# A four-tap convolution moved from diagonal matrices on TensorE to products on ScalarE and sums on GpSimd, and row loads moved to SP's queue

## The chip, the cores and the metric

The kernel runs on one core of a Trainium2 chip. The core has a matrix engine (TensorE, called PE in the profile, with its weight loads as PEld), a vector engine (VectorE, DVE), an activation engine (ScalarE, ACT), a general engine (GpSimd, POOL) and a sequencer that here only issues DMAs (SyncE, SP). Each works through its own queue in order; semaphores tie the queues together. The metric is device time in microseconds (us) of one execution. Lower is better.

## The reference, cut to what matters

The program is a chain of four blocks on x of shape 8 x 512 x 256, all in float32, each added to its input: latent attention, a feed-forward block with 4-bit quantisation, a Mamba block that runs in both directions, and the same feed-forward block again. The change lies in the Mamba block:

```python
h = _layernorm(x, gamma, beta)
xs, z = jnp.split(h @ in_w, 2, axis=-1)              # 512 channels each
y_fwd = _ssm_dir(xs, conv_w, ...)                    # and once more on xs[:, ::-1]
...
# _ssm_dir:
xc = silu(causal_depthwise_conv(xs, conv_w, conv_b)) # four taps per channel
dt, B_ssm, C_ssm = split(xc @ xproj_w, [64, 80])     # 64, 16 and 16 columns
dt = softplus(dt @ dt_w + dt_b)
dA = exp(dt[..., None] * A);  dBu = dt[..., None] * B_ssm[:, :, None, :] * xc[..., None]
h = dA * h + dBu                                     # along time, 16 states per channel
y = einsum('bdn,bn->bd', h, C_ssm) + xc * D_skip
```

So every channel gets a convolution of four taps over time, with a bias and a silu, in each of two directions. B and C are 16 rows each over the 512 time steps, and every channel needs all of them.

## The kernel before, in words

Channels lie on the 128 partitions and time (T = 512) along the free axis. The 512 channels are four tiles of 128 (m = 0 to 3). The work of the eight batch entries b is written as three threads: attention (`thread_a`), the feed-forward blocks together with the front and the end of Mamba (`thread_b`), and the scan (`thread_s`). Their steps are interleaved, so the scan of batch b runs beside the attention of batch b+3 and the Mamba front of batch b+1. The scan of batch 0 can only begin when the attention, the feed-forward block and the Mamba front of batch 0 are done.

The order on every engine is not that of the program text. At the end `issue_in_order` (L138) plans the whole kernel: it takes a cost for each instruction, a rank from what depends on it, and rings of buffers per tag, and writes an order for each engine, SP included. The engines then run these orders as they stand, each instruction waiting for its semaphores, with all that is queued after it.

The Mamba front is `mamba_pre` (L929 on). For each m, PE multiplies by in_w, ACT writes the result to one of two constant tiles `xs` with three columns of zeros on either side (L953), and `conv` (L917) runs once for each direction d. There are 8 x 4 x 2 = 64 convolutions. Before the change a convolution loads four 128 x 128 diagonal matrices (`dg`, 256 KB) from DRAM, where `prep_mamba` has put them at the start (L910 to L915); PE multiplies the four shifted views of xs by them, summing in PSUM (L924); ACT takes a tanh of half the sum and adds 1 (L925, L926); DVE makes the last product from PSUM (L927). The result goes to DRAM (`scr["xc"]`, L958). The tiles `dg` and the result both come from the ring tmpB, which has three buffers (TC = 3).

`ssm_prep` loads the convolved channels back (L1012), multiplies by xproj_w, and writes the 32 rows of B and C to DRAM as `bcd` (L1021). It also makes dt; four of its steps are long operations on POOL.

The scan (`ssm`, L1064) goes over d, m and pairs of states n, 512 times in all. One iteration multiplies u by the two B rows on DVE (L1079), has ACT make two exponentials in PSUM (L1082), scans twice on DVE (L1084 forward, L1086 backward), multiplies by the two C rows on POOL (L1093), and has PE sum over states by transposes (L1096). The B rows and the C rows of a pair, spread over all partitions, are 512 KB each; `load_rep` (L1052) loads them into the rings rep0 and rep1 of three buffers, two iterations ahead. With CQ = 0 both are issued from ACT's queue (L1056). The load of a convolved tile for the skip term (L1092) is issued there too. Every other DMA is issued from SP.

Of the kernel before, what the change touches and what calls it, by code (L numbers as in the profile page):

```python
# [11 lines left out]
F32 = mybir.dt.float32  # L12
# [4 lines left out]
AF = mybir.ActivationFunctionType  # L17
ALU = mybir.AluOpType
AX = mybir.AxisListType

P = 128
T = 512
# [6 lines left out]
ND = INNER // P  # L29
NS = 16  # L30
# [31 lines left out]
DMA_LAT = 2300  # L62
# [75 lines left out]
def issue_in_order(tc, traced, rings):  # L138


    ops = [i for i in traced if i.ins or i.outs]
    ops = [i for i in ops if any(True for _ in accesses(i))]
    acc = [list(accesses(i)) for i in ops]
    n = len(ops)
# [14 lines left out]
    turns, owner, waiting, behind, after = {}, {}, {}, [[] for _ in ops], [[] for _ in ops]  # L159
# [16 lines left out]
    succ = [[] for _ in ops]  # L176
# [19 lines left out]
    dma = [type(i).__name__ == "InstDMACopy" for i in ops]  # L196
    rank = [0.0] * n
    for k in reversed(range(n)):
        rank[k] = costs[k][1] * (1.2 if ops[k].engine == mybir.EngineType.DVE else 1) + DMA_LAT * dma[k] + max([rank[j] for j in succ[k] + behind[k]], default=0.0)
    at = [0.0] * n  # L200
    ready, later, free, last, gone, taken = {}, {}, {}, {}, {}, 0.0
    lines, flying = [0.0] * 16, [0.0] * 8
# [65 lines left out]
def tile_hybrid(ctx: ExitStack, tc: tile.TileContext, w: dict, consts: bass.AP, out: bass.AP):  # L268
    nc = tc.nc
# [14 lines left out]
    def const(shape, dt, tag):  # L284
        return cp.tile(shape, dt, tag=tag, name=tag)
# [7 lines left out]
    def work(shape, dt, tag, bufs=2):  # L293
        cnt[0] += 1
        return ringed(tag, bufs, wk.tile(shape, dt, tag=tag, name=f"{tag}_{cnt[0]}", bufs=bufs))
# [4 lines left out]
    def psum(tag="pb"):  # L300
        cnt[0] += 1
        tag = BMAP.get(tag, tag)
        return ringed(tag, BANKS[tag], ps.tile([P, 512], F32, tag=tag, name=f"{tag}_{cnt[0]}", bufs=BANKS[tag]))
# [559 lines left out]
    Dh = const([P, 2, ND], F32, "Dh")  # L863
    cw = const([P, 2, ND, 4], F32, "cw")
    cb = const([P, 2, ND], F32, "cb")
    cbh = const([P, 2, ND], F32, "cbh")
    dg_d = dr.tile([2, ND, P, 4, P], F32, tag="dgd", name="dg_d", bufs=1)
    TH = T // 2
    xsb = [const([P, 3 + T + 3], F32, f"xs{i}") for i in range(2)]
    for i in range(2):  # L870
# [4 lines left out]
    def prep_mamba():  # L875
        gb = work([P, 2, 2], F32, "gb", 1)
        nc.sync.dma_start(gb[:, 0, :], w["gamma"].rearrange("(a p) -> p a", p=P), allow_slow_non_contiguous=True)
        nc.sync.dma_start(gb[:, 1, :], w["beta"].rearrange("(a p) -> p a", p=P), allow_slow_non_contiguous=True)
        o = psum()
        win = [work([P, 2 * INNER], F32, "dt", NDT) for _ in range(2)]  # L880
        for ct in range(2):
            nc.sync.dma_start(win[ct], w["in_w"][ct * P : (ct + 1) * P, :])
        for m in range(8):
            for ct in range(2):
                PE.matmul(o[:, m : m + 1], win[ct][:, m * P : (m + 1) * P], gb[:, 1, ct : ct + 1],
                          start=(ct == 0), stop=(ct == 1))
        V.tensor_copy(bin_, o[:, :8])
        V.tensor_scalar(binh, bin_, 0.5, None, ALU.mult)
        for ct in range(2):
            V.tensor_scalar(win[ct], win[ct], gb[:, 0, ct : ct + 1], None, ALU.mult)  # L890
            nc.sync.dma_start(win_d[:, :, ct, :].rearrange("m p n -> p m n"), win[ct].rearrange("p (m n) -> p m n", m=8))
        wout = work([P, ND, C], F32, "rep0", RB)
        nc.sync.dma_start(wout, w["out_w"].rearrange("(a p) n -> p a n", p=P))
        V.tensor_scalar(wout, wout, 0.5, None, ALU.mult)
        nc.sync.dma_start(wout_d, wout)
        for d, sx in enumerate(("", "_b")):
            wxp = work([P, 2, T], F32, "tmpA", TA).rearrange("p a t -> p (a t)")[:, : ND * 96].rearrange("p (m n) -> p m n", m=ND)
            nc.sync.dma_start(wxp, w["xproj_w" + sx].rearrange("(a p) n -> p a n", p=P))
            V.tensor_scalar(wxp, wxp, 0.5, None, ALU.mult)
            V.tensor_scalar(wxp[:, :, DTR : DTR + NS], wxp[:, :, DTR : DTR + NS], 0.5, None, ALU.mult)  # L900
            nc.sync.dma_start(wxp_d[d], wxp)
            nc.sync.dma_start(Aneg[:, d], w["A_log" + sx].rearrange("(a p) n -> p a n", p=P))
            nc.sync.dma_start(Dh[:, d, :], w["D_skip" + sx].rearrange("(a p) -> p a", p=P), allow_slow_non_contiguous=True)
            nc.sync.dma_start(cw[:, d], w["conv_w" + sx].rearrange("(a p) k -> p a k", p=P))
            nc.sync.dma_start(cb[:, d, :], w["conv_b" + sx].rearrange("(a p) -> p a", p=P), allow_slow_non_contiguous=True)
        S.activation(Aneg, Aneg, AF.Exp)
        V.tensor_scalar(Aneg, Aneg, -1.0, None, ALU.mult)
        V.tensor_scalar(Dh, Dh, 0.5, None, ALU.mult)
        V.tensor_scalar(cbh, cb, 0.5, None, ALU.mult)
        for d in range(2):  # L910
            for m in range(ND):
                dg = work([P, 4, P], F32, "tmpB", TC)
                for k in range(4):
                    S.activation(dg[:, k, :], ident, AF.Copy, scale=cw[:, d, m, k : k + 1])
                nc.sync.dma_start(dg_d[d, m], dg)  # L915

    def conv(d, m, xs, dst):  # L917

        dg = work([P, 4, P], F32, "tmpB", TC)
        nc.sync.dma_start(dg, dg_d[d, m])  # L920
        o = psum()
        for k in range(4):
            at = k if d == 0 else 6 - k
            PE.matmul(o, dg[:, k, :], xs[:, at : at + T], start=(k == 0), stop=(k == 3))  # L924
        S.activation(dst, o, AF.Tanh, bias=cbh[:, d, m : m + 1], scale=0.5)  # L925
        S.activation(dst, dst, AF.Identity, bias=1.0)  # L926
        V.scalar_tensor_tensor(dst, o, cb[:, d, m : m + 1], dst, ALU.add, ALU.mult)  # L927

    def mamba_pre(src, scr):  # L929
        xn = work([P, NT, C], F32, "fxn", 1)  # L930
# [74 lines left out]
    def ssm_prep(b, d, c, scr):  # L1005

        sx = ("", "_b")[d]
        if c == 0:
            us = []
            for i in range(2):  # L1010
                us.append(work([P, 2, T], F32, "u", NU))
                nc.sync.dma_start(us[i], scr["xc"][4 * d + 2 * i : 4 * d + 2 * i + 2].rearrange("m p t -> p m t"))  # L1012
            wxp = work([P, 2, T], F32, "tmpA", TA).rearrange("p a t -> p (a t)")[:, : ND * 96].rearrange("p (m n) -> p m n", m=ND)
            nc.sync.dma_start(wxp, wxp_d[d])
            o = psum("a")
            for m in range(ND):
                mm(o[:96, :], wxp[:, m, :], us[m // 2][:, m % 2, :], start=(m == 0), stop=(m == ND - 1))
            S.copy(dbt[:DTR, :], o[:DTR, :])
            S.copy(dbt[96:, :], o[DTR:96, :])
            bcd = dr.tile([NS, 2, T], F32, tag="bcd", name=f"bcd_{b}_{d}", bufs=4)  # L1020
            nc.sync.dma_start(bcd.rearrange("n k t -> k n t"), dbt[96:, :])  # L1021
            fronts[(b, d)] = us, bcd
            yield
        us, bcd = fronts[(b, d)]
        u = us[c]
        wdt = work([DTR + 1, 2 * P], F32, "wdt", 1)
        cs = slice(2 * c * P, (2 * c + 2) * P)
        nc.sync.dma_start(wdt[:DTR, :], w["dt_w" + sx][:, cs])
        nc.sync.dma_start(wdt[DTR : DTR + 1, :], w["dt_b" + sx][cs].rearrange("(o n) -> o n", o=1))
        dt = work([P, 2, T], F32, "dt", NDT)  # L1030
        prep[(b, d, c)] = dt, u, bcd
        ex = work([P, 2, T], F32, "tmpA", TA)
        for e in range(2):
            o = psum("a")
            PE.matmul(o, wdt[:, e * P : (e + 1) * P], dbt[: DTR + 1, :], start=True, stop=True)
            S.activation(dt[:, e, :], o, AF.Relu)
            S.activation(ex[:, e, :], o, AF.Abs)
            yield
        S.activation(ex, ex, AF.Exp, scale=-1.0)
        lg = work([P, 2, T], F32, "tmpA", TA)  # L1040
        S.activation(lg, ex, AF.Ln, bias=1.0)
        yield
        G.tensor_tensor(dt, dt, lg, ALU.add)
        S.activation(lg, ex, AF.Identity, bias=1.0)
        S.activation(lg, lg, AF.Identity, bias=neg1[:, 0:1])
        yield
        G.tensor_tensor(ex, ex, lg, ALU.subtract)
        G.tensor_tensor(dt, dt, ex, ALU.add)
        G.tensor_tensor(u, dt, u, ALU.mult)
        yield  # L1050

    def load_rep(b, d, m, n, k):  # L1052

        rep = work([P, 2, T], F32, f"rep{k}", RB)
        src = fronts[(b, d)][1][2 * n : 2 * n + 2, k, :]
        (S, nc.sync)[CQ * k].dma_start(rep, src[None].to_broadcast([P, 2, T]))  # L1056
        return rep

    todo_rep = [(b, d, m, n) for b in range(B) for d in range(2) for m in range(ND) for n in range(NS // 2)]
    todo_c = list(todo_rep)  # L1060
    reps, repc = [], []
    CQ = 0

    def ssm(b, d, scr):  # L1064


        for m in range(ND):
# [8 lines left out]
            for n in range(NS // 2):  # L1076
# [12 lines left out]
                    repc.append(load_rep(*todo_c.pop(0), 1))  # L1089
                if n == 2:  # L1090
                    xp = work([P, T], F32, "xp", 1)
                    S.dma_start(xp, scr["xc"][4 * d + m])  # L1092
                G.tensor_tensor(h, h, rc, ALU.mult)  # L1093
                for e in range(2):
                    for i in range(NT):
# [143 lines left out]
```

## Time and profile before

| | us |
|---|---|
| median of 3 runs | 4006.74 (4004.24 to 4007.3) |
| the profiled execution, own time | 4021.45 |
| its span, first to last instruction | 4019.6 |
| first and last L1079 (scan) | 604.3 and 3884.1 |
| first and last L924 (convolution) | 497.0 and 3461.4 |

| engine | busy us | share of the span | instructions |
|---|---|---|---|
| PE | 3217.1 | 80% | 12964 |
| PEld | 1838.2 | 46% | 12964 |
| DVE | 2957.9 | 74% | 3803 |
| ACT | 1738.8 | 43% | 2989 |
| POOL | 2107.4 | 52% | 1714 |

The mean granted clock of TensorE was 0.872 of full speed. The DMA engines moved 898.12 MB in 570642 packets, with a mean busy share of 0.70.

The busy time is that of instructions that compute. Issuing a DMA and waiting for a semaphore hold an engine's queue but do not count as busy. A row of the groups gives a line of the code, the engine, the operation, out<-in by tile names, shapes and count, then the busy time in us with the mean of one in ns, then the idle time of the engine just before these instructions and what ended most of it. A wait is put down to what ended it, by the semaphores of this one execution. The slices cut the span into 40 equal parts of about 100 us; a digit is a tenth of busy time. PE's matmuls overlap, so their mean duration is longer than their share of the busy time.

### The profile page before, as it was taken

Reading aid. Unit: us, or ns where it says so; the run is one execution under the profiler, and the core shown is the slowest. Engines: PE = TensorE matmul, PEld = TensorE weight load, DVE = VectorE, ACT = ScalarE, POOL = GpSimd, SP = SyncE. Lnnn points to the kernel's source line nnn. Section 1 sums busy time; section 2 is a strip of 40 time slices with the busy share of each in tenths; the row PEclk is TensorE's granted clock in tenths of the full one; section 3 lists DMA queues with packets and bytes.
Section 4 is the critical chain, followed back from the end, with each engine's and each line's share of the span. In section 5 each row is a group of like instructions: output and inputs, shape, how many; then the busy total and the mean of one; then the engine's idle time right before and its main releaser. Section 6 shows DMA issues by size and latency. Waiting matters only on the chain. (4 is left out here: it accounts for less than half of the span.)

```text
span 4019.6 us, 42636 instructions
## 1 busy us (share of the span) xinstructions
PE 3217.1 (80%) x12964; PEld 1838.2 (46%) x12964; DVE 2957.9 (74%) x3803; ACT 1738.8 (43%) x2989; POOL 2107.4 (52%) x1714
## 2 busy tenths in 40 slices
PE   5888997988879878798879888788878767767676
PEld 2333444544544545345444554445444544444543
DVE  5223427778988779886988779886799888879773
ACT  2112344455555344553455444643455445534421
POOL 4112225455766456654665445654576666657542
PEclk7668998999979989899889889899789878887888
DMA  6212357679778877789778886778668877995952
GB/s 162 64 61 70 91 159 245 185 247 297 234 254 253 285 235 222 235 244 303 220 227 259 255 274 187 257 237 288 220 219 274 298 250 231 306 330 183 343 166 67
DMA packets 570642, 898.12 MB, mean 223 GB/s; under 512 B 64781, under 2 KB 219822, under 8 KB 570414
## 3 DMA queue, kind: packets, MB, share of 16 engines
q10 hardware_dynamic: 287744, 553.72, 42.4%
q1 hardware_dynamic: 282670, 341.68, 27.1%
q8 instruction: 104, 1.70, 0.2%
q14 instruction: 124, 1.02, 0.1%
HBM read 783.61 MB, written 103.15 MB: 221 GB/s over the span
## 5 line engine op out<-in xcount | busy, mean ns | idle before, releaser
L1093 POOL TENSOR_TENSOR h<-h,rep 128x1024 f32<-128x1024 f32 x512 | 1216.3, 2381 | 902.8 <-DVE h L1086 346.7
L1082 ACT ACTIVATE a<-dt,Aneg 128x512 f32<-128x512 f32 x1024 | 695.6, 689 | 621.0 <-DVE h L1084 233.8
L1096 PE MATMUL y<-cst,h 128*128 128x128 f32 x4096 | 692.5, 297 | 187.7 <-POOL h L1093 187.4
L1079 DVE TENSOR_TENSOR h<-ub,rep 128x1024 f32<-128x1024 f32 x512 | 615.0, 1207 | 173.6 <-PE y L1096 65.4
L1096 PEld LDWEIGHTS y<-cst,h 128*128 128x128 f32 x4096 | 527.2, 153 | 416.7 <-POOL h L1093 241.0
L1086 DVE TENSOR_TENSOR_SCAN h<-a,h 128x512 f32<-128x512 f32 x512 | 601.5, 1207 | 78.1 <-ACT a L1082 70.0
L1084 DVE TENSOR_TENSOR_SCAN h<-a,h 128x512 f32<-128x512 f32 x512 | 602.0, 1206 | 45.7 <-ACT a L1082 39.7
L696 PE MATMUL pa<-pt,vs 128*32 128x128 f32 (+3 forms) x1024 | 404.5, 495 | 24.2 <-ACT pt L691 22.4
L311 PE MATMUL pb<-wgu,fxT 128*128 128x512 f32 (+1 forms) x768 | 371.8, 593 | 27.2 <-DVE hff L801 12.7
L311 PE MATMUL pb<-qv,hff 128*128 128x256 f32 x1024 | 312.5, 432 | 86.5 <-DMA qv<-sy 73.5
L691 ACT ACTIVATE pt<-pa 128x512 f32<-128x512 f32 x320 | 190.3, 595 | 410.4 <-PE pa L688 358.6
L924 PE MATMUL pb<-xs,tmpB 128*128 128x512 f32 x512 | 266.1, 641 | 26.6 <-DMA tmpB<-dg_d 8.3
L655 PE MATMUL pa<-kst,qst 96*128 96x512 f32 (+3 forms) x512 | 219.8, 470 | 79.4 <-DVE mx L665 51.1
L686 PE MATMUL pa<-qst,kst 98*128 98x512 f32 (+3 forms) x512 | 240.4, 474 | 53.2 <-ACT pt L691 49.5
L311 PEld LDWEIGHTS pb<-qv,hff 128*128 128x128 f32 x1024 | 200.5, 215 | 140.1 <-issue 61.9
L311 PE MATMUL pb<-wdn,hT 128*128 128x256 f32 (+1 forms) x768 | 230.6, 421 | 19.2 <-ACT hT L818 7.1
L665 DVE TENSOR_REDUCE mx<-pa 128x1 f32<-128x512 f32 (+2 forms) x384 | 179.4, 500 | 66.7 <-PE pa L657 66.0
L686 PEld LDWEIGHTS pa<-qst,kst 98*128 98x128 f32 x512 | 108.3, 211 | 244.9 <-issue 125.3
L311 PEld LDWEIGHTS pb<-wgu,fxT 128*128 128x128 f32 x768 | 133.5, 199 | 125.5 <-issue 78.5
L655 PEld LDWEIGHTS pa<-kst,qst 96*128 96x128 f32 x512 | 109.6, 216 | 149.6 <-DVE mx L665 49.0
L311 PEld LDWEIGHTS pb<-wdn,hT 128*128 128x128 f32 (+1 forms) x768 | 141.6, 205 | 72.7 <-issue 27.8
L311 PE MATMUL pa<-xT,wp 128*128 128x512 f32 x256 | 152.6, 712 | 9.3 <-ACT vs L546 3.7
(215 smaller groups left out, 4720.3 us busy)
## 6 DMA issues: line engine op xcount, KB each, us to landing
rep<-bcd ACTq DMA_DIRECT2D x1024, 512.0 KB
hld<-hl SPq DMA_DIRECT2D x64, 512.0 KB
hff<-in_merge_w SPq DMA_DIRECT2D x128, 256.0 KB
qv<-sy SPq DMA_DIRECT2D x128, 256.0 KB
kst<-hld SPq DMA_DIRECT2D x192, 128.0 KB
qst<-hld SPq DMA_DIRECT2D x192, 128.0 KB
tmpB<-dg_d SPq DMA_DIRECT2D x64, 256.0 KB
sxc<-tmpB SPq DMA_DIRECT2D x64, 256.0 KB
```

Of the source, the lines that this page charges most:

```text
L311: PE.matmul(o, L, R, start=start, stop=stop, **kw)
L655: PE.matmul(o[:, at : at + n], qst[pr][:96, j, i * P : (i + 1) * P], kst[:96, j, :n], start=(k == 0), stop=False)
L686: PE.matmul(o[:, at : at + n], kst[:, j, kt * P : (kt + 1) * P], qst[pr][:, j, kt * P :], start=(k == 0), stop=False)
L691: S.activation(pt, o, AF.Exp)
L696: PE.matmul(po[c : c + 32, kt * P :], vs[:, kt, h * VW : h * VW + 32], pt[:, at : at + n], start=(kt == 0), stop=(kt == 2), tile_position= ...
L924: PE.matmul(o, dg[:, k, :], xs[:, at : at + T], start=(k == 0), stop=(k == 3))
L1079: V.tensor_tensor(h, ub[:, None, :].to_broadcast([P, 2, T]), rb, ALU.mult)
L1082: S.activation(a, dt[:, m % 2, :], AF.Exp, scale=Aneg[:, d, m, 2 * n + e : 2 * n + e + 1])
L1084: V.tensor_tensor_scan(h[:, e], a, h[:, e], 0.0, ALU.mult, ALU.add)
L1086: V.tensor_tensor_scan(h[:, e, ::-1], a[:, ::-1], h[:, e, ::-1], 0.0, ALU.mult, ALU.add)
L1093: G.tensor_tensor(h, h, rc, ALU.mult)
L1096: PE.matmul(y[:, i * P : (i + 1) * P], h[:, e, i * P : (i + 1) * P], ident, start=(n == 0 and e == 0 and i == 0), stop=(n == NS // 2 - 1 a ...
```

## The change

A convolution is now a product of the first view of xs with its tap, plus the bias, on ACT; three more products on ACT, each followed by a sum on POOL; a tanh on ACT from SBUF; and one step on DVE from two SBUF tiles. It takes five buffers of the ring tmpB (the result, three products and the tanh). PE, the diagonals, their preparation, their DRAM tensor and their loads are gone. The 32 rows of B and C lie in DRAM one after the other, B first, so the two rows of a pair are one run of 4 KB, where they were two runs of 2 KB. The loads of these rows, and the load at L1092, are issued from SP. The planner's code is the same but for a constant written as 1.0; its order is another one, since the instructions differ. Line numbers after this fall by up to nine.

```diff
-    cbh = const([P, 2, ND], F32, "cbh")
-    dg_d = dr.tile([2, ND, P, 4, P], F32, tag="dgd", name="dg_d", bufs=1)
...
-        V.tensor_scalar(cbh, cb, 0.5, None, ALU.mult)
-        for d in range(2):
-            for m in range(ND):
-                dg = work([P, 4, P], F32, "tmpB", TC)
-                for k in range(4):
-                    S.activation(dg[:, k, :], ident, AF.Copy, scale=cw[:, d, m, k : k + 1])
-                nc.sync.dma_start(dg_d[d, m], dg)
 
     def conv(d, m, xs, dst):
 
-        dg = work([P, 4, P], F32, "tmpB", TC)
-        nc.sync.dma_start(dg, dg_d[d, m])
-        o = psum()
-        for k in range(4):
+        at = 0 if d == 0 else 6
+        S.activation(dst, xs[:, at : at + T], AF.Identity, bias=cb[:, d, m : m + 1], scale=cw[:, d, m, 0:1])
+        for k in range(1, 4):
             at = k if d == 0 else 6 - k
-            PE.matmul(o, dg[:, k, :], xs[:, at : at + T], start=(k == 0), stop=(k == 3))
-        S.activation(dst, o, AF.Tanh, bias=cbh[:, d, m : m + 1], scale=0.5)
-        S.activation(dst, dst, AF.Identity, bias=1.0)
-        V.scalar_tensor_tensor(dst, o, cb[:, d, m : m + 1], dst, ALU.add, ALU.mult)
+            t = work([P, T], F32, "tmpB", TC)
+            S.activation(t, xs[:, at : at + T], AF.Copy, scale=cw[:, d, m, k : k + 1])
+            G.tensor_tensor(dst, dst, t, ALU.add)
+        th = work([P, T], F32, "tmpB", TC)
+        S.activation(th, dst, AF.Tanh, scale=0.5)
+        V.scalar_tensor_tensor(dst, th, 1.0, dst, ALU.add, ALU.mult)
...
-            bcd = dr.tile([NS, 2, T], F32, tag="bcd", name=f"bcd_{b}_{d}", bufs=4)
-            nc.sync.dma_start(bcd.rearrange("n k t -> k n t"), dbt[96:, :])
+            bcd = dr.tile([2 * NS, T], F32, tag="bcd", name=f"bcd_{b}_{d}", bufs=4)
+            nc.sync.dma_start(bcd, dbt[96:, :])
...
     def load_rep(b, d, m, n, k):
 
         rep = work([P, 2, T], F32, f"rep{k}", RB)
-        src = fronts[(b, d)][1][2 * n : 2 * n + 2, k, :]
-        (S, nc.sync)[CQ * k].dma_start(rep, src[None].to_broadcast([P, 2, T]))
+        src = fronts[(b, d)][1][k * NS + 2 * n : k * NS + 2 * n + 2, :].rearrange("n t -> (n t)")
+        nc.sync.dma_start(rep.rearrange("p n t -> p (n t)"), src[None].to_broadcast([P, 2 * T]))
         return rep
...
-    CQ = 0
...
                     xp = work([P, T], F32, "xp", 1)
-                    S.dma_start(xp, scr["xc"][4 * d + m])
+                    nc.sync.dma_start(xp, scr["xc"][4 * d + m])
```

More of the change, by code (lines that the diff above doesn't have):

```diff
@@ L198, in issue_in_order @@
     for k in reversed(range(n)):
-        rank[k] = costs[k][1] * (1.2 if ops[k].engine == mybir.EngineType.DVE else 1) + DMA_LAT * dma[k] + max([rank[j] for j in succ[k] + behind[k]], default=0.0)
+        rank[k] = costs[k][1] * (1.2 if ops[k].engine == mybir.EngineType.DVE else 1.0) + DMA_LAT * dma[k] + max([rank[j] for j in succ[k] + behind[k]], default=0.0)
     at = [0.0] * n
```

## The prediction

> **What bounds the kernel now.** I read the page's busy line and slices first, then busy time by stage, then the waits, then rows by shape for prices.
>
> ```profile
> PE 3217.1 (80%) x12964; PEld 1838.2 (46%) x12964; DVE 2957.9 (74%) x3803; ACT 1738.8 (43%) x2989; POOL 2107.4 (52%) x1714
> PE   5888997988879878798879888788878767767676
> DVE  5223427778988779886988779886799888879773
> POOL 4112225455766456654665445654576666657542
> PEclk7668998999979989899889889899789878887888
> ```
> No engine is full. PE leads until about 600 us, then PE and DVE run side by side at seven to nine tenths. By stage (columns: length; busy us of PE, PEld, DVE, ACT, POOL with counts; clock, DMA share, GB/s):
>
> ```profile
> 604.00:3179.00 2575.00, 2147.76 (x9038) 1223.46 (x9038) 2120.02 (x2637) 1251.50 (x2120) 1507.09 (x1146) 0.90 0.77 247
> 3179.00:3884.00 705.00, 487.91 (x2044) 332.93 (x2042) 583.91 (x637) 306.35 (x485) 435.26 (x291) 0.83 0.79 268
> ```
> The scan stage starts at 604 (first L1079) and holds 3280 us. DVE is busy 82% of the first stretch with PE at 83%, and 83% of the second with PE at only 69%. So PE's load alone does not explain DVE's idle time; orders written out by hand tie the queues together. DVE's work (2704 of 3280 us) is the floor there. Adding up the idle column of DVE's groups over these 3280 us, its 576 us idle ended on PE 195, ACT 194, DMA 92, POOL 34; the rest is small. The waits that matter:
>
> ```profile
> DVE h L1086 <- ACT a L1082: 70.0, 52, 5.9
> DVE tmpB L927 <- ACT tmpB L926: 69.2, 23, 21.5
> DVE h L1079 <- DMA rep<-bcd: 43.4, 21, 4.3
> DVE h L1079 <- issue: 35.7, 17, 6.4
> DVE h L1084 <- ACT a L1082: 39.7, 45, 2.7
> ```
> The rows that price the change (shape; busy, mean ns; idle before), and the present issue of the rep loads:
>
> ```profile
> L924 PE MATMUL pb<-xs,tmpB 128*128 128x512 f32 x512 | 266.1, 641 | 26.6 <-DMA tmpB<-dg_d 8.3 <-DVE h L1086 7.9 <-ACT a L1082 3.8
> L926 ACT ACTIVATE tmpB<-tmpB 128x512 f32<-128x512 f32 x64 | 40.3, 630 | 2.1 <-POOL nrqf L482 0.3
> L927 DVE SCALAR_TENSOR_TENSOR tmpB<-pb,cb,tmpB 128x512 f32<-128x512 f32 x64 | 47.3, 739 | 70.4 <-ACT tmpB L926 69.2 <-DMA tmpB<-dg_d 1.2
> L965 DVE SCALAR_TENSOR_TENSOR tmpB<-tmpB,tmpB 128x512 f32<-128x512 f32 x32 | 39.1, 1223 | 1.6 <-ACT tmpB L964 1.4
> L614 POOL TENSOR_TENSOR tmp<-tmp,tmp 128x512 f32<-128x512 f32 x32 | 41.1, 1283 | 2.0
> L1056 ACTq DMA_DIRECT2D rep<-bcd x1024: 365/366/1542, 588.6 to 3874.8; - x171
> ```
> The later seven groups of convolutions stand in windows of about 110 us each; together:
>
> ```profile
> sum 777.00, PE 629.65 PEld 326.78 DVE 662.84 ACT 421.36 POOL 489.98; mean PE 89.95 PEld 46.68 DVE 94.69 ACT 60.19 POOL 70.00
> ```
> There DVE is at 85%, PE 81%, POOL 63%.
>
> **The change in engine time.** The 64 convolutions lose 512 matmuls (266 us of PE, 0.52 each as they overlap, and 95 us of PEld), 64 loads and 8 stores of diagonals, and 32 small activations of the preparation. On ACT, 683 + 630 ns become five activations at L926's 630: +1.84 x 64 = +118 us. POOL gets 192 sums at 1.27 (L614's median) = +244 us. DVE's last step reads two SBUF operands instead of PSUM. 1088 issues at 0.366 leave ACT: -398 us; the recorded semaphore waits of L1056, 82 us, go with them. SP goes from 1857 DMAs to 1857 - 72 + 1088 = 2873; it is idle most of the time now. What lies on the path:
>
> (a) Start, before 604. The eight convolutions of batch 0 finish between 504 and 598, one per 12-13 us, while PE is busy 101 of 107 us and POOL 24. As sums, POOL needs 24 x 1.27 = 30 us for all eight. DVE does nearly the same work before its first L1079 (437 instructions against 445). The scan could start up to 35 us earlier; PE must still do its other work, so I take -25. Bounds -35 and +10 (one more convolution period). The prepared diagonals are hidden under the first 100 us, where ACT is 29% busy; uncovered they would be 32 x 0.389 = 12 us, counted as 0.
>
> (b) PE in the scan stage loses 7/8 of 266 = 233 of 2636 us. DVE's waits on PE there are 195 us. The two stretches above say that less PE load need free nothing (bound 0); the other bound is 60% of 195, -117. I take a quarter, -49, because the matmuls go from windows where PE is at 81%.
>
> (c) ACT's occupation falls from (1558 + 398 + 82)/3280 = 62% to (1558 + 103)/3280 = 51%. DVE's scans wait 70.0 + 39.7 = 110 us for exponentials that queue behind those issues. Bounds 0 and -110; 40%: -44.
>
> (d) The loads behind SP's other DMAs. Behind each load up to 1.8 others stand on SP, many of which wait for an engine (L958, the store of a convolution, waits 212 us for L927 in 38 cases, longest 21). Pairing issues with their L1079, a B row is issued 12.4 us before use in the middle case, so waits of a few us are covered. DVE's waits for rep, with the unexplained ones, are 79 us: they could vanish (-79) or double (+79). The data, by queue (q10 is ACT's, q1 SP's; packets, MB, share of 16 engines):
>
> ```profile
> q10 hardware_dynamic: 287744, 553.72, 42.4%
> q1 hardware_dynamic: 282670, 341.68, 27.1%
> ```
> q10 spends about 95 ns on a packet, the semaphore writes counted in; packets of 2 KB have a median of 84 ns in the DMA records and those of 4 KB 159, so half as many of 4 KB save little. The 64 loads of diagonals are 16.8 of 898 MB. I take -10.
>
> (e) DVE's last step: L965 is the same form, +0.484 x 64 = +31. Bounds: its minimum of 662 ns, -5; L730 at 128x512, 1469 ns, +47.
>
> (f) Other DVE operations with that contention. L729, L730, L731, L965 (some 326 instructions) run up to 2.9 us against minima near 0.4 to 0.9. POOL is busy 6.1% more of the span, half a sum is 0.63 us: 326 x 0.061 x 0.63 = +13. Bounds 0 and +20.
>
> (g) POOL in the seven windows: 490 + 7 x 24 x 1.27 = 703 of 777 us, 90%; DVE 663 + 27 = 690, 89%. An engine can run at 95% here (DVE, 1000 to 1100 us), so the lower bound is 0. Keeping the busiest at today's 85% needs 703/0.853 = 824, +47. If POOL still waits for DVE 24% of the window (its idle on DVE is 790 of 3280 us), it needs 703 + 186 = 889, +112. I take +30, near the middle of the first two.
>
> Sum: -25 - 49 - 44 - 10 + 31 + 13 + 30 = -54 us. The profiled execution took 4021.45 us (span 4019.6), 14.7 above the median; against the median it is 4006.74 - 54 = 3953 us.
>
> **Waits added.** Each sum waits for a product on ACT; behind it on POOL stand L1093's products, for which PE's transposes wait. ACT's tanh waits for the third sum, and a convolution now takes five tmpB buffers from a ring of three, so products wait for sums too; behind them on ACT stand the exponentials, behind those DVE's scans. Their price has no row in this trace; it is what spans (g) from 0 to +112 and (c) from -110 to 0. DVE's own wait for the tanh (28.6 us in the scan stage for L926 today) I leave as it is: the chain is 3.8 us longer, but the planner places the step later.
>
> **Two rules weighed.** The last step is blocked in L965's row, 662 ns at best, 1223 in the mean. The Trainium skill (SBUF — State Buffer, "Who interferes with whom") says that a VectorE instruction with two SBUF inputs and a reading GpSimd instruction lock each other out for a whole instruction. By that rule, with POOL at 90%, a step waits some 0.8 us, (e) is +46 by my estimate, and the sum -39. Second, the clock was 0.90 at 83% PE and 0.83 at 69%: by these rows seven points less PE cost 0.035 of clock, about 95 us of PE time, which is why (b) is small. TensorE: Matmul & The Clock Gate (Part 1) has only full and half clock, half after an idle window of about 3.4 us: a removed group of four (2.1 us) would leave the clock alone, and the sum would be nearer -120.
>
> **Rivals.**
> A, slower: POOL bounds the seven windows. For it: 90% there, and ACT's tanh, with exponentials behind, waits on POOL. Against: POOL's average stays at 58%. With (g) +112 and (c) 0: -54 + 82 + 44 = +72, 4079 us. It decides once the windows stretch by 84 us together, 12 each.
> B, slower: SP's queue delays rep loads. For: SP's long waits; against: the 12.4 us lead. (d) at +79: +35, 4042 us.
> C, no change: the edit acts, but DVE's floor absorbs it; (b) and (c) halve: -8, 3999 us.
> D, much faster: PE was the true partner in every window; (b) -117 and (c) -70: -148, 3859 us.
>
> **How the numbers follow.** Forecast 0.37, D 0.17, A 0.24, B 0.12, C 0.10. About 0.2% (8 us) is what a measurement here can tell. C is split over the signs: faster 0.57, same 0.06, slower 0.37. The forecast's own range is 3905 to 3995; 3850 to 4080 takes in D and A's point and leaves out their outer halves.
>
> **What would show it.** Right: first scan product before 590 us; DVE busy near 3000, POOL near 2350, PE near 2950; DVE's waits on exponentials near 65 us; rep waits not above 80. Wrong: POOL above 95% in the convolution windows, ACT's tanh waiting on sums by more than 100 us, DVE waiting for rep over 150 us, or a clock below 0.83.

## The result, and the profile after

The changed kernel took 4016.01 us in the median of 20 runs (3995.76 to 4029.76), the kernel before, run beside it, 4003.28 us (3983.4 to 4015.22). The ratio is 1.0033, with a 95% interval of 1.0018 to 1.0047: slower by a third of a percent. The forecast was 3953 us, faster.

A warning for what follows: the profiled execution of the changed kernel took 4000.05 us, 16 us below its median, while that of the kernel before lay 18 us above the median of these 20 runs. So the two profiles differ by -21 us where the medians differ by +13. They show which terms moved; the 34 us between them are no effect of the change.

The busy line and the slices of the changed kernel:

```profile
PE 3045.2 (76%) x12452; PEld 1786.9 (45%) x12452; DVE 3026.6 (76%) x3802; ACT 1847.9 (46%) x3149; POOL 2382.2 (60%) x1906
PE   4878878877877878688777887688785767566776
DVE  5214358888889878797778968896788988789873
POOL 4102355686578557674568646675568667867652
PEclk7778989987888988799887998789786788787888
```
DVE went up by 69 us, POOL by 275, ACT by 109. PE went down by 172 us, not by the 266 of the removed matmuls. The row of the scan's transposes, 4096 before and after, shows where half of the difference went:

```profile
L1096 PE MATMUL y<-cst,h 128*128 128x128 f32 x4096 | 692.5, 297 | 187.7 <-POOL h L1093 187.4
L1087 PE MATMUL y<-cst,h 128*128 128x128 f32 x4096 | 737.0, 311 | 297.5 <-POOL h L1084 292.2 <-DMA hff<-in_merge_w 4.5
```
The mean granted clock fell from 0.872 to 0.846, and the matmuls that stayed took 94 us more. The scan stage, before and after (columns: length; busy us of PE, PEld, DVE, ACT, POOL with counts; clock, DMA share, GB/s):

```profile
604.00:3884.00 3280.00, 2635.67 (x11079) 1556.39 (x11078) 2703.93 (x3273) 1557.85 (x2605) 1942.35 (x1437) 0.89 0.78 251
569.00:3867.00 3298.00, 2516.93 (x10675) 1526.37 (x10675) 2771.29 (x3281) 1663.28 (x2776) 2186.88 (x1606) 0.85 0.74 246
```
It starts 35 us earlier and is 18 us longer. DVE's idle time in it fell from 576 to 527 us, its busy time rose from 2704 to 2771. By the idle columns of its groups, PE ended 135 us of that idle time (194 before), but ACT 200 (194), DMA 97 (92) and POOL 53 (34): about half of what PE no longer ended changed its name. DVE's waits that answer to those shown before, with the wait on the transposes, which is not among those (first line, before the change):

```profile
DVE h L1079 <- PE y L1096: 65.4, 31, 7.7
DVE h L1070 <- PE y L1087: 38.7, 25, 3.7
DVE h L1070 <- DMA rep<-bcd: 74.8, 27, 10.5
DVE h L1077 <- ACT a L1073: 56.4, 52, 3.6
DVE tmpB L919 <- ACT tmpB L918: 41.8, 23, 9.1
DVE h L1075 <- ACT a L1073: 35.2, 39, 4.8
DVE h L1070 <- issue: 16.8, 14, 2.3
```
The scans wait 92 us for exponentials (110 before), and the waits on rep, with the idle time that no semaphore explains (`issue`), are 92 us (79 before). The rows of the new convolution, and the loads:

```profile
L919 DVE SCALAR_TENSOR_TENSOR tmpB<-tmpB,tmpB 128x512 f32<-128x512 f32 x64 | 93.5, 1461 | 41.9 <-ACT tmpB L918 41.8
L916 POOL TENSOR_TENSOR tmpB<-tmpB,tmpB 128x512 f32<-128x512 f32 x192 | 245.2, 1277 | 86.9 <-ACT tmpB L915 56.8
L1048 SPq DMA_DIRECT2D rep<-bcd x1024: 319/320/1711, 547.3 to 3857.6; - x171
```
DVE's last step went from 739 to 1461 ns. An issue takes 0.32 us on SP. That is the longer run and not the queue: in the runs below it is 0.326 us on ACT with runs of 4 KB (rows4k), and 0.370 on SP with runs of 2 KB (sp2k).

### The profile page after: what moved, and what is told of

The parts are those of the page before. It is cut to its first block, busy times and chain, and to the rows that moved or that the text cites. A ratio compares the mean times of both kernels' runs of the same rounds, so it can differ in the third digit from the quotient of the medians.

```text
span 3998.3 us, 41871 instructions
## 1 busy us (share of the span) xinstructions
PE 3045.2 (76%) x12452; PEld 1786.9 (45%) x12452; DVE 3026.6 (76%) x3802; ACT 1847.9 (46%) x3149; POOL 2382.2 (60%) x1906
## 5 line engine op out<-in xcount | busy, mean ns | idle before, releaser
L1084 POOL TENSOR_TENSOR h<-h,rep 128x1024 f32<-128x1024 f32 x512 | 1232.3, 2412 | 720.9 <-DVE h L1075 227.1
L1087 PE MATMUL y<-cst,h 128*128 128x128 f32 x4096 | 737.0, 311 | 297.5 <-POOL h L1084 292.2
L1087 PEld LDWEIGHTS y<-cst,h 128*128 128x128 f32 x4096 | 553.0, 160 | 515.2 <-POOL h L1084 365.5
L696 PE MATMUL pa<-pt,vs 128*32 128x512 f32 (+3 forms) x1024 | 400.4, 489 | 30.9 <-ACT pt L691 30.3
L311 PE MATMUL pb<-qv,hff 128*128 128x256 f32 x1024 | 298.5, 422 | 91.0 <-DMA qv<-sy 74.9
L916 POOL TENSOR_TENSOR tmpB<-tmpB,tmpB 128x512 f32<-128x512 f32 x192 | 245.2, 1277 | 86.9 <-ACT tmpB L915 56.8
L311 PE MATMUL pb<-wdn,hT 128*128 128x256 f32 (+1 forms) x768 | 242.7, 440 | 20.0 <-ACT hT L818 6.3
L915 ACT ACTIVATE tmpB<-xs,cw 128x512 f32<-128x512 f32 x192 | 132.6, 714 | 62.6 <-DMA sxc<-tmpB 35.6
```

Source lines behind the costliest of these rows:

```text
L311: PE.matmul(o, L, R, start=start, stop=stop, **kw)
L696: PE.matmul(po[c : c + 32, kt * P :], vs[:, kt, h * VW : h * VW + 32], pt[:, at : at + n], start=(kt == 0), stop=(kt == 2), tile_position= ...
L916: G.tensor_tensor(dst, dst, t, ALU.add)
L1087: PE.matmul(y[:, i * P : (i + 1) * P], h[:, e, i * P : (i + 1) * P], ident, start=(n == 0 and e == 0 and i == 0), stop=(n == NS // 2 - 1 a ...
```

## The experiments

All ratios are to the kernel before, run beside it on the same chip.

| run | ratio | 95% interval |
|---|---|---|
| the change | 1.0033 | 1.0018 to 1.0047 |
| conv_only | 1.0114 | 1.0085 to 1.0142 |
| loads_only | 0.9799 | 0.9771 to 0.9826 |
| rows4k | 1.0038 | 1.0015 to 1.0061 |
| one_tap | 0.9861 | 0.9834 to 0.9887 |
| tanh_psum | 0.9978 | 0.9955 to 1.0002 |
| sbuf_step | 1.0143 | 1.0108 to 1.0179 |
| cq1 | 0.9966 | 0.9941 to 0.9992 |
| sp2k | 0.9832 | 0.9798 to 0.9866 |
| before_lat2250 | 1.0103 | 1.0077 to 1.0129 |
| after_lat2250 | 1.0062 | 1.0032 to 1.0092 |
| conv_only_lat2250 | 1.0196 | 1.0160 to 1.0232 |
| loads_only_lat2250 | 0.9935 | 0.9910 to 0.9961 |
| short_sums | 0.9953 | 0.9924 to 0.9982 |
| short_step | 1.0006 | 0.9977 to 1.0036 |
| short_both | 0.9938 | 0.9911 to 0.9964 |
| short_mm | 0.9989 | 0.9964 to 1.0014 |
| sp_same_order | 0.9860 | 0.9833 to 0.9887 |
| tanh_psum_lat2250 | 0.9960 | 0.9939 to 0.9980 |

### The two halves of the change, apart

**conv_only**: the changed kernel with the layout and the queue of the old loads.

```diff
-            bcd = dr.tile([2 * NS, T], F32, tag="bcd", name=f"bcd_{b}_{d}", bufs=4)
-            nc.sync.dma_start(bcd, dbt[96:, :])
+            bcd = dr.tile([NS, 2, T], F32, tag="bcd", name=f"bcd_{b}_{d}", bufs=4)
+            nc.sync.dma_start(bcd.rearrange("n k t -> k n t"), dbt[96:, :])
...
-        nc.sync.dma_start(rep.rearrange("p n t -> p (n t)"), src[None].to_broadcast([P, 2 * T]))
+        S.dma_start(rep, src[None].to_broadcast([P, 2, T]))
...
-                    nc.sync.dma_start(xp, scr["xc"][4 * d + m])
+                    S.dma_start(xp, scr["xc"][4 * d + m])
```


> Only the convolution changes (products on ScalarE, sums on GpSimd); the B and C rows are loaded as before, in runs of 2 KB from ACT's queue. Theory 1 (the convolution's gains, 35 us at the start and some 60 us of DVE waits on PE, about cancel against 69 us more DVE busy time, and the moved loads cost little): ratio to the kernel before 0.996 to 1.003. Rival (moving the loads to SP is what costs, the convolution alone is a gain): ratio 0.985 to 0.993, and DVE's waits for rep near the 43 us of before. Rival (the convolution on ACT holds the exponentials up, and was only saved by ACT losing its DMA issues): ratio above 1.006, DVE's waits on exponentials above 150 us.

**loads_only**: the kernel before with the reverse of that diff: runs of 4 KB, issued from SP, and the convolution on PE.

> Only the loads change (runs of 4 KB, issued from SP); the convolution stays on TensorE. Theory 1: ratio 0.997 to 1.004, since ACT's freed 400 us of issue time are not on the path. Rival (SP's queue delays rep loads): ratio 1.005 to 1.015 and DVE plus POOL waiting for rep over 150 us. Rival (ACT's issue time was on the path, as the prediction had it): ratio 0.985 to 0.992, DVE's waits on exponentials down from 110 us to about 65.

The halves pull in opposite directions: +1.1% and -2.0%. Both readings that made the loads the smaller matter were wrong. The readings that came nearest in time named signs that did not come: DVE's waits on exponentials were to pass 150 us in conv_only and are 112, and to fall to about 65 in loads_only, where they are 108, against 110 before:

```profile
DVE h L1086 <- ACT a L1082: 58.9, 43, 4.8
DVE h L1084 <- ACT a L1082: 49.4, 44, 3.0
```
The scan stages, conv_only first:

```profile
588.00:3917.00 3329.00, 2528.78 (x10676) 1533.53 (x10675) 2777.30 (x3286) 1667.19 (x2778) 2189.22 (x1611) 0.85 0.75 243
```

```profile
590.00:3803.00 3213.00, 2623.10 (x11083) 1554.54 (x11082) 2699.48 (x3275) 1559.52 (x2604) 1949.86 (x1438) 0.89 0.78 256
```
With the convolution changed DVE works 73 us more than before (2777 against 2704) and the stage is 49 us longer, although PE works 107 us less. With the loads changed no engine's busy time moves by more than 13 us, and the stage is 67 us shorter: DVE's idle time falls from 576 to 514 us. DMA ended 28 us less of it, PE 15, ACT 12.

### Is it the order that was drawn?

Each edit makes the planner write another order, and one_tap, tanh_psum, sbuf_step and cq1 below can't be read before it is known what a new order alone does. So both halves, the change and the kernel before were run again with one constant of the planner altered.

```diff
-DMA_LAT = 2300
+DMA_LAT = 2250
```


> The kernel before with the planner's latency of a DMA at 2250 ns instead of 2300: the same work, another order drawn. It prices the luck of an order. If orders matter little: ratio 0.997 to 1.003. If differences of 1 to 2% can be luck: ratio outside 0.99 to 1.01.

> The changed kernel with the same other latency. If the 1.0033 of the change is the change and not the order: ratio 1.000 to 1.007. If it is luck, it lies elsewhere, 0.985 to 0.997 or above 1.01.

> Only the convolution changed, with the other latency. The convolution's own cost, if it is no luck: 1.008 to 1.015 again. If luck: 0.995 to 1.005.

> Only the loads changed, with the other latency. The gain of moving them to SP, if it is no luck: 0.976 to 0.985 again. If luck: 0.99 to 1.00.

The kernel before lost 1.0% by nothing but another order. So the luck of an order is as large as most effects here. Taken as they stand, loads_only_lat2250 fell into the range that its reading gave to luck, and conv_only_lat2250 above both of its ranges; both ranges had left out that the kernel before would move as well. What holds in both draws, each against the kernel before with the same constant: the loads gain 2.0% (0.9799) and 1.7% (0.9935/1.0103 = 0.983); the convolution costs 1.1% and 0.9% (1.0196/1.0103 = 1.009). The change as a whole is +0.3% in the first and -0.4% in the second (1.0062/1.0103 = 0.996). Its sign belongs to the order. The same constant does not make the same order in two kernels, though, and two draws are few: the loads' gain is larger than this luck and is found again below in an unchanged order; the convolution's 1.1% in the first draw is hardly more than what the kernel before lost by its second (1.0103).

### The loads: issue time, queue, length of the runs

**rows4k**: 4 KB runs, still issued from ACT; the write of bcd is shaped so that every engine keeps its order.

```diff
-            bcd = dr.tile([NS, 2, T], F32, tag="bcd", name=f"bcd_{b}_{d}", bufs=4)
-            nc.sync.dma_start(bcd.rearrange("n k t -> k n t"), dbt[96:, :])
+            bcd = dr.tile([2 * NS, T], F32, tag="bcd", name=f"bcd_{b}_{d}", bufs=4)
+            nc.sync.dma_start(bcd.rearrange("(k n) t -> k n t", k=2), dbt[96:, :])
...
-        (S, nc.sync)[CQ * k].dma_start(rep, src[None].to_broadcast([P, 2, T]))
+        S.dma_start(rep.rearrange("p n t -> p (n t)"), src[None].to_broadcast([P, 2 * T]))
```


> The kernel before with B and C rows laid out so that a pair is one run of 4 KB, still issued from ACT, and with every engine's order the same as before. Theory 1: ratio 0.998 to 1.002; packets on ACT's queue fall from 287744 to about 156700 and their share from 42.4% to 38 to 41%. Rival (the DMA engines are a bound in the merge stages): ratio below 0.997.

The packets nearly halved, the share of the DMA engines hardly moved (42.4% before), and the time rose by 0.4%:

```profile
q10 hardware_dynamic: 156672, 553.72, 41.4%
q1 hardware_dynamic: 282894, 341.68, 27.0%
```
In the changed kernel's DMA records a packet of 4 KB takes 190 ns in the mean, one of 2 KB 104. The longer runs are no gain. They also shorten each issue on ACT by 0.04 us, 41 us in all, and that did not pay either.

**cq1** (C rows alone from SP) and **sp2k** (all of them, in 2 KB runs):

```diff
-    CQ = 0
+    CQ = 1
```


> The kernel before with the C rows loaded from SP and the B rows still from ACT (runs of 2 KB). Theory (each load's issue on ACT costs, through what queues behind it): half of what loads_only gained, ratio 0.986 to 0.994. Rival (it is the B rows alone, which DVE waits for): ratio 0.997 to 1.003. Rival (it is the luck of the new order): any ratio, 0.975 to 1.01, out of step with the count of moved loads.

```diff
-        (S, nc.sync)[CQ * k].dma_start(rep, src[None].to_broadcast([P, 2, T]))
+        nc.sync.dma_start(rep, src[None].to_broadcast([P, 2, T]))
...
-                    S.dma_start(xp, scr["xc"][4 * d + m])
+                    nc.sync.dma_start(xp, scr["xc"][4 * d + m])
```


> The kernel before with all rep loads and the skip loads issued from SP, in runs of 2 KB as before. Since runs of 4 KB from ACT with the same order took 1.0038 of the time, theory: ratio 0.974 to 0.982, a little below loads_only. Rival (the gain of loads_only needs the 4 KB runs, which halve the packets on the one queue left): ratio above 0.985.

Half of the loads gained 0.3%, all of them 1.7%: the right direction, not in proportion, and cq1 less than expected, in orders that differ. **sp_same_order** takes the orders out: sp2k, but the planner treats the moved loads as ACT's, so PE, DVE, POOL and all else on ACT and SP stand in the old order; only the queue that issues them is SP's.

```diff
+    eng = [mybir.EngineType.Activation if type(i).__name__ == "InstDMACopy" and any(x[7] and x[0].startswith("xp") or not x[7] and x[0].startswith("bcd") for x in a) else i.engine
+           for i, a in zip(ops, acc)]
...
-        heapq.heappush(later.setdefault(ops[k].engine, []), (at[k], k))
+        heapq.heappush(later.setdefault(eng[k], []), (at[k], k))
```


> The kernel before with the 1088 loads of B and C rows and skip tiles issued from SP in runs of 2 KB (as sp2k, 0.983), but planned as if they were on ACT, so that PE, DVE, POOL, and ACT's and SP's other instructions stand in the order of the kernel before. If ACT's freed issue time is on the path: ratio 0.978 to 0.990. If the gain comes from the new order: 0.996 to 1.003. If SP's queue delays loads in an order that was not made for it: above 1.003.

0.986: taking these issues off ACT is worth 1.4% by itself, 56 us. With the 398 us of issuing go the waits for buffers that the loads held in ACT's queue (82 us by the prediction's count); the run does not separate the two. DVE's waits of this run, exponentials and rep:

```profile
DVE h L1082 <- DMA rep<-bcd: 72.1, 40, 5.4
DVE h L1089 <- ACT a L1085: 39.5, 33, 4.5
DVE h L1087 <- ACT a L1085: 33.3, 31, 3.3
DVE h L1082 <- issue: 31.7, 17, 8.4
```
The scans' waits on exponentials fell from 110 to 73 us, 37 where the prediction took 44, and all the idle time of DVE in the scan stage that ACT ended from 194 to 145; the scan began at 591.5 us, 13 earlier. The rep waits rose from 79 to 104 us.

### What less TensorE work is worth

**one_tap** leaves out three of the four taps of the convolution on PE, in a new order:

```diff
-        for k in range(4):
-            at = k if d == 0 else 6 - k
-            PE.matmul(o, dg[:, k, :], xs[:, at : at + T], start=(k == 0), stop=(k == 3))
+        PE.matmul(o, dg[:, 3, :], xs[:, 3 : 3 + T], start=True, stop=True)
```


> The kernel before with one of the four taps of each convolution; three of four products are left out, so 384 matmuls (200 us of TensorE busy time) go, and nothing is added on any other engine. Theory 1 (less TensorE work frees about 30% of DVE's waits on PE and about 20 us at the start): ratio 0.980 to 0.988. Rival (DVE's floor and the hand-written orders absorb it, as the two stretches with 83% and 69% TensorE suggest): ratio 0.994 to 1.002. Rival (TensorE is the true partner): ratio below 0.975. The clock should fall from 0.87 to about 0.85.

0.986 lies in the range of the first reading, that less work on PE pays (0.980 to 0.988). But it can be the order's luck, and most of it is not where that reading had it: this kernel's scan begins at 566 us, 38 earlier, and its scan stage, 566 to 3825, is 20 us shorter than before. **short_mm** keeps the order: two of the four products cover 24 columns, and the planner is told that they are 512 wide.

```diff
+        w = T if w == 24 else w
...
-            PE.matmul(o, dg[:, k, :], xs[:, at : at + T], start=(k == 0), stop=(k == 3))
+            n = T if k in (0, 3) else 24
+            PE.matmul(o[:, :n], dg[:, k, :], xs[:, at : at + n], start=(k == 0), stop=(k == 3))
```


> The kernel before, same order on every engine, but two of the four tap products of each convolution cover 24 of 512 columns; their other columns are left out. About 125 us of TensorE go and nothing else. If TensorE's relief is worth what the prediction took (a fifth to a quarter of the time taken off): ratio 0.991 to 0.995. If DVE's floor absorbs it: 0.997 to 1.002. If one_tap's 0.986 was TensorE's relief in full: 0.988 to 0.991.

```profile
PE 3147.3 (79%) x12964; PEld 1827.6 (46%) x12964; DVE 2955.1 (74%) x3803; ACT 1737.9 (43%) x2989; POOL 2109.4 (53%) x1714
L926 PE MATMUL pb<-xs,tmpB 128*128 128x512 f32 x256 | 158.8, 706 | 22.2 <-DMA tmpB<-dg_d 13.5 <-ACT xs L955 4.6 <-ACT fxT L526 2.7
L926 PE MATMUL pb<-xs,tmpB 128*128 128x24 f32 x256 | 39.9, 262 | 0.0
```
The two rows overlap to 186 us together, so 80 us of convolution left PE (not the 125 expected: the 512-wide products that remain overlap less) and 70 us of busy time in all. The ratio is 0.9989, 4 us, with 1 well inside the interval, whose end allows 14 us; the prediction's price, 49 us for 233, would make 17 of these 80. So in this order less work on PE is worth nothing that can be measured, and the prediction's price is just outside. What one_tap gained beyond that can be a better order that the missing work permits, or luck; the runs do not tell which.

### What the sums and the last step cost

**short_sums**, **short_step** and **short_both** keep the order of the changed kernel and shrink its sums, its last step, or both to 24 columns.

```diff
+    if n == 24:
+        n = T
...
-            G.tensor_tensor(dst, dst, t, ALU.add)
+            G.tensor_tensor(dst[:, :24], dst[:, :24], t[:, :24], ALU.add)
...
-        V.scalar_tensor_tensor(dst, th, 1.0, dst, ALU.add, ALU.mult)
+        V.scalar_tensor_tensor(dst[:, :24], th[:, :24], 1.0, dst[:, :24], ALU.add, ALU.mult)
```


> The changed kernel, same order on every engine, but each of the 192 sums on GpSimd covers 24 of 512 columns; the sums over the other 488 are left out. About 200 us of GpSimd go. If the sums are what the convolution costs: ratio to the kernel before 0.985 to 0.994. If DVE's lock on its last step is: the step falls to some 800 to 900 ns as there is less to wait for, and the ratio is 0.993 to 0.998. If neither matters: 1.001 to 1.005, as the changed kernel itself (1.0033).

> The changed kernel, same order, but DVE's last step of each convolution covers 24 of 512 columns; the rest of the product with the tanh is left out. Its 24-column form still asks for two SBUF operands, so it can still wait for GpSimd, but its own work (0.55 us of 0.66) is gone. If DVE's busy time is the floor, microsecond for microsecond: 35 us less, ratio 0.993 to 0.996. If it is the wait and not the work: 0.999 to 1.003.

> Both shortened, same order: what is left of the new convolution is ScalarE's five activations. If the causes add: the two gains summed, ratio 0.978 to 0.988. If the convolution's cost is ScalarE's 118 us: ratio above 0.996.

Against the changed kernel (1.0033), the sums are worth 0.8% (32 us), the last step 0.3% (11 us, within the noise of the two intervals), both 0.95%: they add, within the noise. The waits of the chain stay in these kernels (POOL idles 185 us before the shortened sums, 87 before the full ones), so they are not in this price. The ratio of short_sums lies in the range given to DVE's lock, but the sign of that reading, a step of 800 to 900 ns, did not come. The rows of its sums and of its last step:

```profile
L918 POOL TENSOR_TENSOR tmpB<-tmpB,tmpB 128x24 f32<-128x24 f32 x192 | 45.6, 237 | 184.8 <-ACT tmpB L917 130.6 <-issue 30.9 <-DVE tmpB L921 10.1
L921 DVE SCALAR_TENSOR_TENSOR tmpB<-tmpB,tmpB 128x512 f32<-128x512 f32 x64 | 84.3, 1317 | 27.9 <-ACT tmpB L920 27.8
```
200 us fewer on POOL shortened DVE's step only from 1461 to 1317 ns; it is POOL's other work, above all the scan's products, that the step runs into: 44 of these 64 steps start while POOL is in an instruction, 35 of them in a product of the scan. In short_step the step has almost no work of its own left:

```profile
L921 DVE SCALAR_TENSOR_TENSOR tmpB<-tmpB,tmpB 128x24 f32<-128x24 f32 x64 | 60.6, 946 | 39.3 <-ACT tmpB L920 39.0
```
A product over 24 columns takes 946 ns, 119 at the least. Most of this instruction is waiting, and the trace shows for what: 54 of the 64 start while POOL is in an instruction, and 50 of these end 0.04 us after it ends; the ten others take 173 ns in the mean. In the changed kernel, with 512 columns, it is 52 of 64, of which 50 end 0.55 us after POOL's instruction; they take 1641 ns in the mean, the twelve others 682.

**tanh_psum** takes the wait away in a kernel that computes everything: the tanh goes to PSUM, and the step reads one operand from SBUF.

```diff
-        th = work([P, T], F32, "tmpB", TC)
+        th = psum()
         S.activation(th, dst, AF.Tanh, scale=0.5)
```


> The changed kernel, but the tanh of a convolution is written to PSUM, so that DVE's last step has one operand in SBUF instead of two. Theory (the convolution costs 1.1% because its last step on DVE and GpSimd lock each other out: 1461 ns measured against 739): the step falls to about 740 ns, DVE's busy time by 46 us or more, and the ratio to the kernel before is 0.985 to 0.994. Rival (GpSimd's 244 us of sums delay the scan in the windows, whatever DVE's last step reads): the step falls all the same, ratio 0.998 to 1.004.

> The changed kernel with its tanh in PSUM, in the order drawn with a DMA latency of 2250 ns. The changed kernel in that draw took 1.0062, and with the tanh in PSUM in the first draw 0.9978 against 1.0033. If the lock's cost is real: 0.996 to 1.002. If that gain was the order's luck: 1.004 or more.

```profile
L919 DVE SCALAR_TENSOR_TENSOR tmpB<-pb,tmpB 128x512 f32<-128x512 f32 x64 | 43.3, 677 | 40.2 <-ACT pb L918 40.1
```
The step fell from 1461 to 677 ns (675 in the 48 steps that start while POOL is in an instruction), DVE's busy time from 3026.6 to 2970.0 us, and the time by 0.55% in the first draw and 1.0% in the second (0.9960 against 1.0062). In the first draw the ratio, 0.9978, is at the edge of the rival's range and far from the theory's. The kernel also takes a buffer of tmpB less and has a new order, so its gain is not the lock's alone. With this one line the changed kernel is no slower than the kernel before.

**sbuf_step** put the lock, DVE and GpSimd shutting each other out, into the kernel before: PE's convolution, but a last step from two SBUF tiles.

```diff
-        S.activation(dst, o, AF.Tanh, bias=cbh[:, d, m : m + 1], scale=0.5)
-        S.activation(dst, dst, AF.Identity, bias=1.0)
-        V.scalar_tensor_tensor(dst, o, cb[:, d, m : m + 1], dst, ALU.add, ALU.mult)
+        th = work([P, T], F32, "tmpB", TC)
+        S.activation(th, o, AF.Tanh, bias=cbh[:, d, m : m + 1], scale=0.5)
+        S.activation(dst, o, AF.Identity, bias=cb[:, d, m : m + 1])
+        V.scalar_tensor_tensor(dst, th, 1.0, dst, ALU.add, ALU.mult)
```


> The kernel before with TensorE's convolution, but the sum with its bias is copied to SBUF by ScalarE in place of the step that adds 1, and DVE's last step reads two SBUF tiles. Theory (the last step's lock is the cost): DVE's step goes from 739 to 1200 to 1450 ns, DVE busy +30 to +45 us, ratio 1.006 to 1.012. Rival (GpSimd's sums are the cost): ratio 0.998 to 1.005.

The step came to 1113 ns and the time to 1.014, more than the 24 us of the step (64 x 0.374) can be. This kernel also takes a third buffer per convolution from the ring of three and has a new order, so it is inconclusive on the size.

## Why the prediction was wrong, step by step

The bounds named (DVE's work as the floor of the scan stage, all queues tied by written orders) held. The sum did not. Its terms for the convolution, (a), (b), (e), (f) and (g), add to 0; conv_only measured +46 us, and +37 in the second draw. Its terms for the loads, (c) and (d), add to -54; alone they gained 80 and 67 us, beside the new convolution 32 and 54. The shortfall is among the gains: short_both, with POOL's sums at 47 us instead of 245 and DVE's last steps at 51 instead of 94 (47 before the change), is 25 us faster than the kernel before, where (a) to (d) had 128.

(a) Start, -25: the scan began at 569 instead of 604, -35, at the bound given. Convolutions of batch 0 ended every 9 us instead of every 13. But conv_only began it at 588 and loads_only at 590, so about half came with the loads or the order, and in the second draw it was 580 against 588.

(b) PE's relief, -49: the step that failed. DVE's waits on PE did fall as the prediction took it, from 194 to 135 us, but half of that was not free time: ACT, DMA and POOL ended 29 us more of DVE's idle time. short_mm, in an unchanged order, found 4 us (14 at most) for 80 us of PE's convolution. The prediction had the evidence in hand, DVE idle at 18% and 17% beside PE at 83% and 69%, made it the bound of 0, and then took a quarter of the waits all the same. With (b) at 0, and nothing else mended, the sum is -5 us, about rival C. What the relief is worth where the planner may write another order stays open.

(c) ACT's issues, -44: in the unchanged order of sp_same_order the mechanism is right, and the size near (waits on exponentials from 110 to 73, time -56 us). Other orders show it less: the same waits are 108 in loads_only and 100 in sp2k, which gain more. In the changed kernel they fell only to 92, and ACT was 105 us busier in the scan stage. The prediction had ACT's occupation fall from 62% to 51%, less than a fifth, and yet took 40% of the waits; that the convolution's five activations queue in front of exponentials is likely, but no run prices it. They also take longer than the 630 ns it put in: 710 for a product, 800 for the first. That this queueing is why the loads gain less beside the new convolution, 0.8% (1.0033/1.0114) against 2.0% in the first draw and 1.3% (1.0062/1.0196) against 1.7% in the second, is argued, not shown.

(d) The loads, -10: not confirmed. rep waits rose by 13 us in the changed kernel and by 25 in sp_same_order, but were 80 in loads_only, 68 in sp2k, and in the second draw 52 in the changed kernel against 88 before: they have no steady sign. POOL's waits for its C rows rose from 32 to 95 us. The 4 KB runs, which were to save little, cost 0.4%, 15 us, in an unchanged order.

(e) DVE's last step, +31: measured (1461 - 739) x 64 = +46 us. The nearest row was the right one, but it met POOL less often: POOL is in an instruction at 19 of L965's 32 starts and at 52 of the new step's 64. Where it is, they take 1598 and 1641 ns; where it is not, 676 and 682. The rule of the Trainium skill that the prediction set beside it (SBUF — State Buffer, "Who interferes with whom": the two engines lock each other out for a whole instruction) gave +46 by its estimate, and the 24-column step of 946 ns bears it out.

(f) Other DVE work in the way of POOL, +13: DVE's busy time rose by 69 us, of which 46 are (e); the rows that the prediction named, L729, L730, L731 and L965, took 16 us more (419 before, 435 after).

(g) POOL in the windows, +30: short_sums prices the sums at 32 us, including 9 us of (e), without the waits of the chain. A case as dear as rival A was not there, though its sign came: it was to decide once the windows stretch by 84 us, and the seven, from the first convolution to the last, are 901 us in all now, 124 more. 102 of these are in the first, whose last convolution came late; the other six grew from 667 to 689. POOL is busy 82% of them, not 90%:

```profile
sum 901.00, PE 634.34 PEld 352.23 DVE 779.97 ACT 564.15 POOL 742.62; mean PE 90.62 PEld 50.32 DVE 111.42 ACT 80.59 POOL 106.09
```
PE's transposes wait longer for POOL (292 us, 187 before), but DVE's wait on those transposes went down, from 65 to 39 us. Of the waits added, ACT's tanh waited 36 us for the sums, and its products 62 us for buffers of tmpB.

The clock behaved as the rows said: it fell by 0.026 where the prediction had 0.035, and PE's other work took 94 us more where it had 95. (The sign "PE near 2950" leaves this out; it was 3045.) That 95 was worked out on the scan stage alone, from the larger fall, so that the two agree so closely is luck. The Trainium skill (TensorE: Matmul & The Clock Gate, Part 1) gives the clock of a single busy core two states, full, and half after an idle window of about 3.4 us. The traces agree: every record of the granted clock is 1.0 or 0.5, and the stretches at half are mostly of 3.4 or 6.8 us. What did not hold is the prediction's inference that taking out groups of 2.1 us would leave the clock alone: the time at half clock went from 1032 to 1231 us.

In short: the loads on SP are a gain of 1.7 to 2.0%, 1.4% in an unchanged order. The convolution on ScalarE and GpSimd is a loss of about 1% in both draws, which is as much as the luck of an order; the 0.95% that short_both takes back, in an unchanged order, is what supports it. The two do not add up undisturbed. The fastest kernel computing everything was loads_only at 0.9799, the change without its convolution, and sp2k stands beside it at 0.9832.

## What to carry to other kernels

Take time off an engine only where something waits for it last: a wait that ends on that engine is no gain by itself, since the next engine may end it a little later. To price such a relief, shrink the operation and keep every queue's order; where a planner writes the order, run each verdict in a second draw, for a new order alone moved this kernel by 1%. Issue DMAs from a queue with nothing else to do, and let a VectorE step that runs beside a busy GpSimd read one of its operands from PSUM.

## What was not expected of the hardware

Issuing 1088 DMAs from ACT, about 0.366 us each, and waiting for their buffers there cost 1.4% of the kernel in an unchanged order, though ACT computed only 43% of the time. Doubling the run of a DMA's packets to 4 KB brought nothing: 190 ns in the mean against 2 x 104. An operation of DVE over 24 columns, 119 ns at the least, took 946 in the mean, since it ended only when the instruction of GpSimd that it met had ended. And with 266 us of dense matmuls gone, TensorE spent 199 us more at half clock, its mean granted clock fell from 0.872 to 0.846, and its other work took back a third of the 266, 94 us.
